# A two-layer graph attention kernel: scores of a chunk in two groups of 32 nodes, 640 slots each

## The chip, the cores and the metric

The kernel runs on one core of a Trainium2 chip. The metric is the time of one execution on the device in microseconds (us). TensorE (PE) multiplies matrices and loads their stationary operand (PEld), VectorE (DVE) and ScalarE (ACT) work element by element, GpSimd (POOL) issues the gathers, and SyncE (SP) issues most of the other transfers.

## The reference, cut to what matters

Two layers of attention over the edges of a graph with 6250 nodes of 128 features and 106250 edges, which come sorted by their destination. Layer normalisation of `x` plus the result stands at the end.

```python
def _transformer_conv(h, edge_attr, src, dst, Wq, bq, Wk, bk, Wv, bv, We, Ws, bs):
    q = (h @ Wq + bq).reshape(n, H, C)              # H = 2 heads of C = 64
    k = (h @ Wk + bk).reshape(n, H, C)
    v = (h @ Wv + bv).reshape(n, H, C)
    e = (edge_attr @ We).reshape(-1, H, C)          # 32 time features and 64 message features
    alpha = jnp.einsum('ehc,ehc->eh', q[dst], k[src] + e) / jnp.sqrt(C)
    a = segment_softmax(alpha, dst)                 # over all edges of one destination
    out = segment_sum((v[src] + e) * a[:, :, None], dst)
    return out.reshape(n, H * C) + h @ Ws + bs

edge_attr = concatenate([cos((node_vec[src] - edge_weight) * time_w + time_b), edge_attr_64])
h = _transformer_conv(x, edge_attr, ...)            # first layer
h = relu(batchnorm(h))
out = layernorm(x + _transformer_conv(h, edge_attr, ...))
```

## The kernel before

The sorted edges are cut into NC = 106 chunks. A chunk has CE = 1024 slots (T = 8 tiles of P = 128 edges) and a window of NN = 64 destination nodes, so NN nodes times H = 2 heads make 128 rows of scores. A plan at the start finds the first node and the first slot of each chunk, tests whether all chunks fit, and writes the flag `oki`; on it the program branches into `ordered` (measured here) or a general path.

`conv(c, ...)` runs twice (c = 0 and 1), each time as a software pipeline over rounds k, written out by hand in the loop at L937. In a round each step works on another chunk:

- `fetch(k + 4)` and `gather(k + 4)`: loads of the chunk's edge features into the tile `ff` and of its score tables `ftab` (SP's queue), and eight indirect gathers (POOL, L749), one for each tile of 128 edges, of source rows (`xv_d`, or `h_d` and `hn_d` in the second convolution) into `ff`.
- `turn_in(k + 1, u)`: PE turns the gathered rows (L799), in the first convolution also the edge features (L811); ACT copies them to `fft` and `fet`. In the second convolution the turned edge features are loaded from `et_d` instead. The first turn of a chunk waits for all eight gathers.
- `score(k, u)`: PE computes all 128 rows against 1024 slots in two halves of 512 (L822, L823) into `fps`. Slots of other nodes are masked by large codes in the tables.
- `lowest(k)` and `weigh(k)`: DVE takes the minimum of each row (L828), ACT the exponential (L835) into `fs`.
- `turn_weights(k - 1)`: PE turns the eight tiles of weights (L845), ACT copies them to `fpt` (L846).
- `gather_sums(k - 1)`: PE adds up weights times features, eight matmuls of 225 columns into `fpa` (L852).
- `divide(k - 2)`, `finish_turn(k - 2)`, `apply(k - 2)`, `finish(k - 2)`: division by the sum of weights (DVE), two turns (L872, L873) and a copy `fat` (L875), the value matrices (L882, L883 or L888, L889), and the end: the result's columns go to `hT` (L900), or in the second convolution the layer normalisation, whose rows `store` writes.
- `pull(extra, ...)`: one step of a generator `rest()`: in the first convolution the score tables of later nodes (`tables`, L627) and, when the last chunk of a block of 512 nodes is done, `pass_rows`, which turns that block of `hT` (L1015) and writes it to `h_d`; in the second convolution the tables of the second layer.

Each engine executes its instructions in the order in which they are issued. `ff` and `ftab` have six buffers, `fps`, `fpa` and `fpo` one each. Between the two convolutions all of `hT` must be done for the batch statistics; the second convolution's first gathers read `h_d`. Its chunk 105 ends with the store of the last rows.

Of the kernel before, what the change touches and what calls it, by code (L numbers as in the profile page):

```python
# [13 lines left out]
P = 128  # L14
# [33 lines left out]
NC = 106  # L48
EW = ED + 1

BITS = 8
# [609 lines left out]
def ordered(ctx: ExitStack, tc: tile.TileContext, pl, x, dst, edge_attr_64, conv2, bn_g, bn_b, out):  # L661
# [37 lines left out]
    def conv(c, extra, first_blocks=None):  # L699
# [13 lines left out]
        together = mybir.DependencyInfo(mybir.DependencyClass.Sync, mybir.DependencyReason.DATA)  # L713
        ets = [pl.xT[:EC, i * CE:(i + 1) * CE] for i in range(AHEAD + 2)]
        ch = {}
        norm = [None, None, None]
# [3 lines left out]
        def fetch(k):  # L720
            s = ch[k] = Plan()
            lo, hi = first(k)
            s.nb = nc.sync.value_load(pl.nbs[0:1, k:k + 1], min_val=lo, max_val=hi)
            sl = nc.sync.value_load(pl.sls[0:1, k:k + 1], min_val=0, max_val=E - CE)
            s.f = f = load.tile([P, T, FW], F32, name="ff")
            nc.sync.dma_start(f[:, :, 1 + D + TD:D + EW],
                              edge_attr_64[bass.ds(sl, CE), :].rearrange("(t p) d -> p t d", p=P))
            if c:
                nc.vector.memset(f[:, :, D + EW:1 + D + EW], 1.0)
            else:  # L730
                bits = small.tile([P, T, BITS], I32, name="fbits")
                nc.vector.tensor_tensor(bits, pl.dsts[:, :, k:k + 1].to_broadcast([P, T, BITS]),
                                        pl.bitm[:, None, :].to_broadcast([P, T, BITS]), OP.bitwise_and)
                nc.vector.tensor_scalar(f[:, :, D + EW:D + EW + BITS], bits, 0.0, None, op0=OP.is_equal)
                nc.vector.tensor_copy(f[:, :, D + EW + BITS:], bits)
            s.tab = load.tile([P, NN * H, 3 - c], F32, name="ftab")
            nc.sync.dma_start(s.tab, pl.tab_d[c][:, bass.ds(s.nb, NN)].rearrange("p n h w -> p (n h) w"))
            if c:
                s.z = load.tile([P, T, TD], F32, name="fz", bufs=AHEAD)
                nc.sync.dma_start(s.z, enc_d[k].rearrange("p (t d) -> p t d", d=TD))  # L740
                s.et = ets[k % len(ets)]
                nc.sync.dma_start(s.et, et_d[k])
                s.r = load.tile([NN, D], F32, name="fr", bufs=AHEAD + 3)
                nc.sync.dma_start(s.r, res_d[bass.ds(s.nb, NN), :])
# [70 lines left out]

        def score(k, u):

            s = ch[k]
            if u == 0:
                s.ps = p_s.tile([P, CE], F32, name="fps")  # L820
            w = slice(u * GE, (u + 1) * GE)
            nc.tensor.matmul(s.ps[:, w], s.tab[:, :, 0], s.ft[:, w], start=True, stop=False)  # L822
            nc.tensor.matmul(s.ps[:, w], s.tab[:EC, :, 1], s.et[:, w], start=False, stop=True)  # L823

        def lowest(k):
            s = ch[k]
            low = small.tile([P, 1], F32, name="flow")
            nc.vector.tensor_reduce(low, s.ps, AX.X, OP.min)  # L828
            s.bias = small.tile([P, 1], F32, name="fm")
            nc.vector.tensor_scalar(s.bias, low, HIGHEST, None, op0=OP.min)  # L830

        def weigh(k):
            s = ch[k]
            s.s = work.tile([P, CE], F32, name="fs")
            nc.scalar.activation(s.s, s.ps, AF.Exp, bias=s.bias, scale=-1.0)  # L835

        def turn_weights(k):

            s = ch[k]
            s.pt = work.tile([P, CE], F32, name="fpt")  # L840
            for u in range(2):
                pp = p_tr.tile([P, GE], F32, name="fppt", tag="tr")
                for t in range(4):
                    at = u * GE + t * P
                    nc.tensor.transpose(pp[:, t * P:(t + 1) * P], s.s[:, at:at + P], ident)  # L845
                nc.scalar.copy(s.pt[:, u * GE:(u + 1) * GE], pp)  # L846

        def gather_sums(k):
            s = ch[k]
            s.pa = p_a.tile([P, D + EW], F32, name="fpa")  # L850
            for t in range(T):
                nc.tensor.matmul(s.pa, s.pt[:, t * P:(t + 1) * P], s.f[:, t, 1:1 + D + EW], start=t == 0, stop=t == T - 1)  # L852

# [81 lines left out]

        with cs, tc.manual_schedule():
            for k in range(-AHEAD, NC + 3):  # L937
                def on(j):
# [5 lines left out]
                if k == -AHEAD and c:  # L944
                    first_blocks()
                if on(k):
                    score(k, 0)
                if on(k - 1):
# [4 lines left out]
                if on(k):  # L953
                    score(k, 1)
                if on(k - 2):
                    finish_turn(k - 2)
                if on(k):
                    lowest(k)
                if on(k + 1):
                    turn_in(k + 1, 0)  # L960
                if on(k - 2):
                    apply(k - 2)
                if on(k):
# [164 lines left out]
def tile_gnn_resnorm(ctx: ExitStack, tc: tile.TileContext, x, src, dst, edge_attr_64, edge_weight, node_vec,  # L1128
# [3 lines left out]
    E = src.shape[0]  # L1132
    step = -(-E // NC)
    keep = ctx.enter_context(tc.tile_pool(name="keep", bufs=1))
    made = ctx.enter_context(tc.tile_pool(name="made", bufs=1, space=bass.MemoryType.DRAM))
# [6 lines left out]
    with tc.tile_pool(name="plan", bufs=1) as pl, tc.tile_pool(name="planw", bufs=2) as mw, \  # L1142
# [3 lines left out]
        for r0, r1 in ((0, R // 16 * 16), (R // 16 * 16, R)):  # L1146
            nc.sync.dma_start(win[r0:r1], bass.AP(tensor=dst.tensor, offset=dst.offset + step * (r0 + 1) - (P - 1),
                                                  ap=[[step, r1 - r0], [1, P]]))
# [23 lines left out]
        tau_i = pl.tile([P, 1], I32, name="tau_i")  # L1172
        nc.gpsimd.iota(tau_i, pattern=[[0, 1]], base=step, channel_multiplier=step)
        lane_i = pl.tile([P, 1], I32, name="lane_i")
# [62 lines left out]
        nc.vector.tensor_scalar(span[:, 1], span[:, 1], float(CE), None, op0=OP.is_gt)  # L1237
        bad = pl.tile([1, 4], F32, name="bad")
        nc.vector.tensor_scalar(bad[:, 3:], ends[:, 0, NC - 2:NC - 1], N - NN + 0.5, None, op0=OP.is_gt)
        nc.vector.tensor_reduce(bad[:, 0:1], span, AX.XY, OP.add)  # L1240
# [97 lines left out]
```

## Time and profile before

| | |
|---|---|
| median of 14 runs | 2286.08 us (2283.77 to 2289.91) |
| the profiled execution | 2286.73 us, its span 2284.9 us |
| busy: PE, DVE, ACT, POOL | 2202.6, 1226.9, 1225.3, 1620.7 us |
| gathers of the first convolution (POOL) | first at 38.06, last at 1127.37 us |
| gathers of the second convolution (POOL) | first at 1181.08, last at 2244.96 us |
| score matmuls, L822 and L823, x1696 | 442.8 + 218.1 + 217.8 us busy |
| turns of weights, L845, x1696 | 220.0 us busy |
| sums, L852, x3392 | 681.9 us busy |

The span runs from the first instruction to the last; what lies around it makes the profiled execution 1.8 us longer. A logical matmul of 4-byte numbers appears as two instructions, a turn as one. The ends of matmuls are modelled and overlap the next start, so their pace is read from start to start. In a line of a timeline the columns are the start, the length, the engine, the line of the kernel, the operation, the tiles written and read with their shapes, how many in a row, and in brackets how long the engine had been idle and what released it. In a group of the page: the sum of busy time, the mean in ns, and the idle time before, with what ended most of it.

### The profile page before, as it was taken

Reading aid. Unit: us, or ns where it says so; the run is one execution under the profiler, and the core shown is the slowest. Engines: PE = TensorE matmul, PEld = TensorE weight load, DVE = VectorE, ACT = ScalarE, POOL = GpSimd, SP = SyncE. Lnnn points to the kernel's source line nnn. Section 1 sums busy time; section 2 is a strip of 40 time slices with the busy share of each in tenths; the row PEclk is TensorE's granted clock in tenths of the full one; section 3 lists DMA queues with packets and bytes.
Section 4 is the critical chain, followed back from the end, with each engine's and each line's share of the span. In section 5 each row is a group of like instructions: output and inputs, shape, how many; then the busy total and the mean of one; then the engine's idle time right before and its main releaser. Section 6 shows DMA issues by size and latency. Waiting matters only on the chain.

```text
span 2284.9 us, 39797 instructions
## 1 busy us (share of the span) xinstructions
PE 2202.6 (96%) x11586; PEld 1704.2 (75%) x11586; DVE 1226.9 (54%) x3738; ACT 1225.3 (54%) x1955; POOL 1620.7 (71%) x1717
## 2 busy tenths in 40 slices
PE   5999999999999999999979999999999999999997
PEld 3687878878887888888856777777777777777765
DVE  5576767676666666777735443344343334433333
ACT  3677777766566666555643343444444444444444
POOL 3777777767777777777527777777777777777772
PEclk8899999999999999999998999999999999999999
DMA  7666666656665666666539666666666766656561
GB/s 235 172 185 163 180 187 182 183 145 184 185 176 168 174 188 176 178 173 172 159 100 255 178 180 180 172 189 178 188 181 163 192 188 175 184 163 164 161 162 27
DMA packets 431119, 396.64 MB, mean 174 GB/s; under 512 B 279697, under 2 KB 375182, under 8 KB 427566
## 3 DMA queue, kind: packets, MB, share of 16 engines
q1 hardware_dynamic: 357680, 239.73, 38.3%
q0 software_dynamic: 54656, 113.07, 19.0%
q10 hardware_dynamic: 18558, 41.20, 5.2%
q8 instruction: 98, 1.61, 0.3%
q14 instruction: 127, 1.04, 0.2%
HBM read 277.19 MB, written 113.17 MB: 171 GB/s over the span
## 4 chain that ended last, share of the span: by engine, by line
PE 90%; DVE 3%; DMA 2%; issue 2%; POOL 2%; ACT 1%; SPq 0%; ACTq 0%; DVEq 0%; POOLq 0%
PE fpa L852 28%; PE fps L822 16%; PE fps L823 15%; PE fppt L845 8%; PE fpx L799 7%; PE fpg L627 4%; PE fpe L811 4%; PE fpo L888 2%; DVE fat L875 2%; POOL ff L749 2%; PE fpo L889 1%; PE fpo L882 1%; PE fpo L873 1%; PE fpo L872 1%; PE fpo L883 1%
## 5 line engine op out<-in xcount | busy, mean ns | idle before, releaser
L749 POOL DMA_INDIRECT ff<-xv_d,fsrcs x848 | 811.4, 957 | 305.8 <-issue 230.4
L749 POOL DMA_INDIRECT ff<-hn_d,fsrcs x824 | 781.5, 948 | 253.4 <-issue 221.9
L852 PE MATMUL fpa<-ff,fpt 128*128 128x225 f32 x3392 | 681.9, 353 | 0.0
L852 PEld LDWEIGHTS fpa<-ff,fpt 128*128 128x128 f32 x3392 | 634.6, 190 | 52.3 <-issue 48.5
L846 ACT COPY fpt<-fppt 128x512 f32<-128x512 f32 x424 | 228.2, 590 | 448.2 <-PE fppt L845 423.9
L822 PE MATMUL fps<-fft,ftab 128*128 128x512 f32 x848 | 442.8, 604 | 1.7 <-ACT fs L835 1.7
L806 ACT COPY fft<-fpx 128x512 f32<-128x512 f32 x418 | 243.3, 582 | 365.0 <-PE fpx L799 358.4
L875 DVE COPY fat<-fpo 128x256 f32<-128x256 f32 x212 | 90.1, 425 | 599.0 <-PE fpo L873 581.5
L835 ACT ACTIVATE fs<-fps,fm 128x1024 f32<-128x1024 f32 x212 | 236.4, 1115 | 76.4 <-DVE fm L830 69.8
L845 PEld LDWEIGHTS fppt<-fident,fs 128*128 128x128 f32 x1696 | 198.4, 140 | 104.8 <-issue 104.2
L799 PE MATMUL fpx<-fident,ff 128*128 128x128 f32 x1696 | 263.2, 278 | 13.9 <-ACT fo L631 5.3
L828 DVE TENSOR_REDUCE flow<-fps 128x1 f32<-128x1024 f32 x212 | 257.6, 1215 | 8.3 <-PE fps L823 8.3
L845 PE MATMUL fppt<-fident,fs 128*128 128x128 f32 x1696 | 220.0, 272 | 0.0
L823 PE MATMUL fps<-fxT,ftab 112*128 112x512 f32 x424 | 218.1, 595 | 0.4 <-DMA fxT<-et_d 0.4
L823 PE MATMUL fps<-fet,ftab 112*128 112x512 f32 x424 | 217.8, 595 | 0.0
L799 PEld LDWEIGHTS fpx<-fident,ff 128*128 128x128 f32 x1696 | 194.7, 142 | 27.0 <-ACT fo L631 7.1
L822 PEld LDWEIGHTS fps<-fft,ftab 128*128 128x128 f32 x848 | 166.7, 226 | 5.5 <-ACT fs L835 3.4
L823 PEld LDWEIGHTS fps<-fet,ftab 112*128 112x128 f32 x424 | 106.4, 251 | 76.1 <-issue 60.2
L823 PEld LDWEIGHTS fps<-fxT,ftab 112*128 112x128 f32 x424 | 83.8, 198 | 100.0 <-issue 97.8
L857 DVE TENSOR_SCALAR finv<-fpa 128x1 f32<-128x1 f32 x212 | 32.0, 151 | 211.0 <-issue 156.8
L774 DVE SCALAR_TENSOR_TENSOR farg<-fturns,farg 128x256 f32<-128x256 f32 x318 | 135.5, 426 | 10.9
L811 PE MATMUL fpe<-fident,ff 128*112 128x128 f32 x848 | 129.1, 275 | 1.5 <-DVE ff L786 1.5
(202 smaller groups left out, 2317.6 us busy)
## 6 DMA issues: line engine op xcount, KB each, us to landing
ff<-in_edge_attr SPq DMA_DIRECT2D x212, 256.0 KB
et_d<-fet SPq DMA_DIRECT2D x106, 448.0 KB
fxT<-et_d SPq DMA_DIRECT2D x106, 448.0 KB
ftab<-tab_d SPq DMA_DIRECT2D x106, 192.0 KB
tab_d<-fo ACTq DMA_DIRECT2D x13, 1536.0 KB
ff<-xv_d,fsrcs POOLq DMA_INDIRECT x848
enc_d<-fzs SPq DMA_DIRECT2D x106, 128.0 KB
ftab<-tab_d SPq DMA_DIRECT2D x106, 128.0 KB
```

What stands on the lines that cost most here:

```text
L749: nc.gpsimd.indirect_dma_start(out=f[:, t, (1 if c else 0):1 + D], out_offset=None, in_=(h_d if k < RAW else hn_d) if c else pl.xv_d, in_o ...
L799: turn = nc.tensor.transpose(px[:, t * P:(t + 1) * P], s.f[:, u * 4 + t, 1:1 + D], ident)
L806: nc.scalar.copy(s.ft[:, u * GE:(u + 1) * GE], px)
L811: nc.tensor.transpose(pe[:EC, t * P:(t + 1) * P], s.f[:, u * 4 + t, 1 + D:], ident)
L822: nc.tensor.matmul(s.ps[:, w], s.tab[:, :, 0], s.ft[:, w], start=True, stop=False)
L823: nc.tensor.matmul(s.ps[:, w], s.tab[:EC, :, 1], s.et[:, w], start=False, stop=True)
L828: nc.vector.tensor_reduce(low, s.ps, AX.X, OP.min)
L835: nc.scalar.activation(s.s, s.ps, AF.Exp, bias=s.bias, scale=-1.0)
L845: nc.tensor.transpose(pp[:, t * P:(t + 1) * P], s.s[:, at:at + P], ident)
L846: nc.scalar.copy(s.pt[:, u * GE:(u + 1) * GE], pp)
L852: nc.tensor.matmul(s.pa, s.pt[:, t * P:(t + 1) * P], s.f[:, t, 1:1 + D + EW], start=t == 0, stop=t == T - 1)
L875: nc.vector.tensor_copy(s.at, s.po)
```

## The change

The 64 nodes of a chunk are taken as two groups of 32. The first group is scored over slots 0 to 639, the second over slots 384 to 1023. Each group has 64 rows, which take 64 columns of TensorE: the first group's results stand on partitions 0 to 63 of `fps`, the second's on 64 to 127. `score` issues eight matmuls of 320 slots that alternate between the groups, in place of four of 512 slots with all 128 columns. Minimum and exponential work on 640 columns. `turn_weights` turns five tiles; four copies put each group's half of the turned tiles to its place among eight tiles of 128 columns, in one of two fixed buffers `pts`, whose other places are zeroed once at the start of each convolution, so that `gather_sums` stays as it is. The plan tests in addition that the border between the groups lies where both fit, which moves the turning of `dst` ahead of `oki`, and shifts the chunks' starts by 68 edges.

The order of a round changes: turning the weights of k - 1 comes first, both halves of the score follow together, `finish` works on chunk k - 3 in place of k - 2 and stands after the score, `finish_turn(k - 2)` comes after the turning in, and `apply(k - 2)` ends the round, after `gather_sums(k - 1)`. `ftab` and `fr` get one buffer more.

```diff
@@ conv @@
+        pts = [work.tile([P, T, P], F32, name=f"fpt{i}", bufs=1) for i in range(2)]
...
-            s.tab = load.tile([P, NN * H, 3 - c], F32, name="ftab")
+            s.tab = load.tile([P, NN * H, 3 - c], F32, name="ftab", bufs=AHEAD + 3)
...
-                s.r = load.tile([NN, D], F32, name="fr", bufs=AHEAD + 3)
+                s.r = load.tile([NN, D], F32, name="fr", bufs=AHEAD + 4)
...
-        def score(k, u):
+        def score(k):
             s = ch[k]
-            if u == 0:
-                s.ps = p_s.tile([P, CE], F32, name="fps")
-            w = slice(u * GE, (u + 1) * GE)
-            nc.tensor.matmul(s.ps[:, w], s.tab[:, :, 0], s.ft[:, w], start=True, stop=False)
-            nc.tensor.matmul(s.ps[:, w], s.tab[:EC, :, 1], s.et[:, w], start=False, stop=True)
+            s.ps = p_s.tile([P, 2, GE], F32, name="fps")
+            for u in range(2):
+                for i, (tab, of) in enumerate(((s.tab, s.ft), (s.tab[:EC], s.et))):
+                    for g in range(2):
+                        at = g * (CE - WE) + u * HE
+                        nc.tensor.matmul(s.ps[g * NN:(g + 1) * NN, u, :HE], tab[:, g * NN:(g + 1) * NN, i],
+                                         of[:, at:at + HE], start=i == 0, stop=i == 1)
...
-            nc.vector.tensor_reduce(low, s.ps, AX.X, OP.min)
+            nc.vector.tensor_reduce(low, s.ps[:, :, :HE], AX.XY, OP.min)
...
-            s.s = work.tile([P, CE], F32, name="fs")
-            nc.scalar.activation(s.s, s.ps, AF.Exp, bias=s.bias, scale=-1.0)
+            s.s = work.tile([P, WE], F32, name="fs")
+            nc.scalar.activation(s.s.rearrange("p (u e) -> p u e", u=2), s.ps[:, :, :HE], AF.Exp, bias=s.bias, scale=-1.0)
...
-            s.pt = work.tile([P, CE], F32, name="fpt")
-            for u in range(2):
+            s.pt = pts[k % 2]
+            for lo, hi in ((0, 4), (4, WT)):
                 pp = p_tr.tile([P, GE], F32, name="fppt", tag="tr")
-                for t in range(4):
-                    at = u * GE + t * P
-                    nc.tensor.transpose(pp[:, t * P:(t + 1) * P], s.s[:, at:at + P], ident)
-                nc.scalar.copy(s.pt[:, u * GE:(u + 1) * GE], pp)
+                for t in range(lo, hi):
+                    nc.tensor.transpose(pp[:, (t - lo) * P:(t - lo + 1) * P], s.s[:, t * P:(t + 1) * P], ident)
+                for g in range(2):
+                    nc.scalar.copy(s.pt[:, lo + g * (T - WT):hi + g * (T - WT), g * NN:(g + 1) * NN],
+                                   pp[:, :(hi - lo) * P].rearrange("p (t m) -> p t m", m=P)[:, :, g * NN:(g + 1) * NN])
...
         with cs, tc.manual_schedule():
+            for pt in pts:
+                nc.vector.memset(pt, 0.0)
             for k in range(-AHEAD, NC + 3):
...
-                if on(k):
-                    score(k, 0)
                 if on(k - 1):
                     turn_weights(k - 1)
                 place()
                 if on(k - 2):
                     divide(k - 2)
                 if on(k):
-                    score(k, 1)
-                if on(k - 2):
-                    finish_turn(k - 2)
+                    score(k)
+                if on(k - 3):
+                    finish(k - 3)
                 if on(k):
                     lowest(k)
                 if on(k + 1):
                     turn_in(k + 1, 0)
-                if on(k - 2):
-                    apply(k - 2)
                 if on(k):
                     weigh(k)
                 if on(k + 1):
                     turn_in(k + 1, 1)
                 if on(k - 2):
-                    finish(k - 2)
+                    finish_turn(k - 2)
...
                 if on(k - 1):
                     gather_sums(k - 1)
+                if on(k - 2):
+                    apply(k - 2)
@@ tile_gnn_resnorm @@
+        columns(flats[1], dsts)
+        split = pl.tile([1, 3, NC], F32, name="split")
+        nc.vector.tensor_scalar(split[:, 0], ends[:, 0, :NC], NH - 0.5, None, op0=OP.add)
+        for i, (t, op) in enumerate(((T - WT, OP.is_gt), (WT, OP.is_lt))):
+            nc.vector.tensor_copy(split[:, 1 + i], dsts[0:1, t])
+            nc.vector.tensor_tensor(split[:, 1 + i], split[:, 1 + i], split[:, 0], op)
+        nc.vector.tensor_reduce(bad[:, 4:], split[:, 1:], AX.XY, OP.add)
         tot = pl.tile([1, 1], F32, name="tot")
         nc.vector.tensor_reduce(tot, bad, AX.X, OP.add)
         nc.vector.tensor_scalar(oki, tot, 0.0, None, op0=OP.is_equal)
-        columns(flats[1], dsts)
         columns(flats[2], ew)
```

WT = 5 tiles, WE = 640 slots, HE = 320 and NH = 32 are new constants.

More of the change, by code (lines that the diff above doesn't have):

```diff
@@ L49 @@
 EW = ED + 1
+WT = 5
+WE = WT * P
+HE = WE // 2
+NH = NN // 2
 BITS = 8
@@ L851, in gather_sums @@
             for t in range(T):
-                nc.tensor.matmul(s.pa, s.pt[:, t * P:(t + 1) * P], s.f[:, t, 1:1 + D + EW], start=t == 0, stop=t == T - 1)
+                nc.tensor.matmul(s.pa, s.pt[:, t], s.f[:, t, 1:1 + D + EW], start=t == 0, stop=t == T - 1)
         def divide(k):
@@ L1133, in tile_gnn_resnorm @@
     step = -(-E // NC)
+    less = NC * step - E
     keep = ctx.enter_context(tc.tile_pool(name="keep", bufs=1))
@@ L1146, in tile_gnn_resnorm @@
         for r0, r1 in ((0, R // 16 * 16), (R // 16 * 16, R)):
-            nc.sync.dma_start(win[r0:r1], bass.AP(tensor=dst.tensor, offset=dst.offset + step * (r0 + 1) - (P - 1),
+            nc.sync.dma_start(win[r0:r1], bass.AP(tensor=dst.tensor, offset=dst.offset + step * (r0 + 1) - less - (P - 1),
                                                   ap=[[step, r1 - r0], [1, P]]))
@@ L1172, in tile_gnn_resnorm @@
         tau_i = pl.tile([P, 1], I32, name="tau_i")
-        nc.gpsimd.iota(tau_i, pattern=[[0, 1]], base=step, channel_multiplier=step)
+        nc.gpsimd.iota(tau_i, pattern=[[0, 1]], base=step - less, channel_multiplier=step)
         lane_i = pl.tile([P, 1], I32, name="lane_i")
@@ L1237, in tile_gnn_resnorm @@
         nc.vector.tensor_scalar(span[:, 1], span[:, 1], float(CE), None, op0=OP.is_gt)
-        bad = pl.tile([1, 4], F32, name="bad")
-        nc.vector.tensor_scalar(bad[:, 3:], ends[:, 0, NC - 2:NC - 1], N - NN + 0.5, None, op0=OP.is_gt)
+        bad = pl.tile([1, 5], F32, name="bad")
+        nc.vector.tensor_scalar(bad[:, 3:4], ends[:, 0, NC - 2:NC - 1], N - NN + 0.5, None, op0=OP.is_gt)
         nc.vector.tensor_reduce(bad[:, 0:1], span, AX.XY, OP.add)
```

## The prediction

> **What bounds the kernel now.** The page first: engine rows and the groups of the gathers.
>
> ```profile
> PE 2202.6 (96%) x11586; PEld 1704.2 (75%) x11586; DVE 1226.9 (54%) x3738; ACT 1225.3 (54%) x1955; POOL 1620.7 (71%) x1717
> L749 POOL DMA_INDIRECT ff<-xv_d,fsrcs x848 | 811.4, 957 | 305.8 <-issue 230.4
> L749 POOL DMA_INDIRECT ff<-hn_d,fsrcs x824 | 781.5, 948 | 253.4 <-issue 221.9
> ```
>
> PE is busy 96%, so shorter scores look like a gain in every round. POOL's 71% hides a second bound: most idle time before a gather is "issue", a wait for nothing visible. The timeline of POOL in the second convolution shows the beat:
>
> ```profile
> 1599.49 0.94 POOL L749 DMA_INDIRECT ff<-hn_d,fsrcs  x1 [0.30 <-issue]
> 1600.74 0.94 POOL L749 DMA_INDIRECT ff<-hn_d,fsrcs  x1 [0.30 <-issue]
> 1601.99 0.95 POOL L749 DMA_INDIRECT ff<-hn_d,fsrcs  x1 [0.30 <-issue]
> ```
>
> One gather per 1.25 us: 0.94 busy, 0.30 until the next. The same beat holds from 38 to 60 us, when PE has hardly started, so it is POOL's own. Eight gathers make a round of 10.0 us. Now PE's round, from its timeline in the first convolution:
>
> ```profile
> 600.88 3.21 PE L852 MATMUL fpa<-ff,fpt 128*128 128x225 f32 x16
> 603.92 1.02 PE L822 MATMUL fps<-fft,ftab 128*128 128x512 f32 x2
> 604.78 1.02 PE L823 MATMUL fps<-fet,ftab 112*128 112x512 f32 x2
> 605.64 1.04 PE L845 MATMUL fppt<-fident,fs 128*128 128x128 f32 x8
> 606.51 1.08 PE L822 MATMUL fps<-fft,ftab 128*128 128x512 f32 x2
> 607.43 1.02 PE L823 MATMUL fps<-fet,ftab 112*128 112x512 f32 x2
> ...
> 610.71 3.21 PE L852 MATMUL fpa<-ff,fpt 128*128 128x225 f32 x16
> ```
>
> Start to start it is 9.83 us; the blocks of `rest()` (0.86 us a matmul, about 58 us per convolution) raise the first convolution above 10.0. So the first is PE's, narrowly. In the second the fpa starts lie 9.38 apart where nothing is added: PE would need 106 x 9.38 + 47 = 1041 us, POOL ran 1181.1 to 2245.9 = 1065. The second is already POOL's. Where PE holds POOL up is in the waits of POOL, and where the end of a convolution is lost is in the timeline:
>
> ```profile
> POOL ff L749 <- PE fpa L852: 32.3, 39, 2.8
> ```
>
> ```profile
> 1127.37 0.94 POOL L749 DMA_INDIRECT ff<-xv_d,fsrcs  x1 [0.30 <-DMA ff<-xv_d,fsrcs]
> 1151.71 0.60 PE L799 MATMUL fpx<-fident,ff 128*128 128x128 f32 x4
> 1181.08 0.94 POOL L749 DMA_INDIRECT ff<-h_d,fsrcs  x1 [52.76 <-ACT fhT L1094]
> 2244.96 0.94 POOL L749 DMA_INDIRECT ff<-hn_d,fsrcs  x1 [0.30 <-issue]
> 2247.77 0.60 PE L799 MATMUL fpx<-fident,ff 128*128 128x128 f32 x4
> ```
>
> Of the 32.3 us, 39 x 0.30 are the usual beat; 20.6 are waits for a freed `ff`. The last chunk's rows are turned at 1151.71, 24.3 us after their last gather began; at the end of the second convolution that takes 2.8. So PE ends the first convolution 21.5 us behind. These two are what a shorter PE round can win; the rest is POOL's beat.
>
> **PE's round after the change.** Out: four score matmuls (two instructions each, start to start 0.43), 4 x 0.863 = 3.45 us, and three turns of 0.109 = 0.33. In: eight logical matmuls over 320 slots into 64 columns. At 0.43 us for 512 slots an instruction takes 0.267; sixteen one after another are S = 4.27. No row of before has matmuls in different column halves, so S is bounded by that and by complete overlap, 2.13. The halves alternate in PE's order; if an instruction of one half runs beside the next of the other, sixteen fit into nine steps: S = 2.40, which I take. The nearest rows are the 64-column matmuls of `apply`:
>
> ```profile
> 2229.13 0.63 PE L799 MATMUL fpx<-fident,ff 128*128 128x128 f32 x4 [0.85 <-DMA ff<-hn_d,fsrcs]
> 2229.68 0.20 PEld L888 LDWEIGHTS fpo<-fwv,fat 128*64 128x64 f32 x2 [0.17 <-issue]
> 2229.85 0.28 PE L889 MATMUL fpo<-fwe,fat 128*64 128x64 f32 x2
> 2230.09 0.28 PE L889 MATMUL fpo<-fwe,fat 128*64 128x64 f32 x2
> 2230.31 0.66 PE L799 MATMUL fpx<-fident,ff 128*128 128x128 f32 x4
> ```
>
> Four instructions pass between 2229.85 and 2230.09, 0.06 each, though each weight load lasts 0.10: loads run beside matmuls in 64 columns too. The turns before and after stand about 0.1 us off: two changes of shape, 0.2 a round. The round is S + 0.55 + 1.74 + 0.22 + 0.44 + 3.04 + 0.2 = S + 6.2: 8.6 instead of 9.8, and the first convolution 106 x 8.6 + 58 = 970 us of PE against 1062 of POOL. PE is ahead of POOL for any S up to about 3.2.
>
> The Trainium skill, "TensorE: Matmul & The Clock Gate", Part 3 (The mechanism), says that a weight load overlaps running matmuls only if its row group differs, and both halves here use all rows. By it sixteen loads of 0.1 would be bare, S = 4.0 and the change slower; the 0.06 pace above contradicts it, and no run yet shows it for two column halves. The same part reports 2.38 times for three column tiles; by that rate two would give, as an estimate, S near 2.7, with the same sum as 2.40.
>
> **The sum, against the profiled execution (run 2286.73, span 2284.9; median 2286.08, 0.65 lower).**
> 1. POOL's waits for `ff` go: 1127.4 becomes 1106.8. A further 8 us of slightly long gathers in the first convolution (957 against 948 ns) may or may not stay; I keep them.
> 2. The last chunk is turned 2.8 us later, at 1109.6, instead of 1151.7: -42.1.
> 3. From there to the last sums: before 20.0 us (1151.7 to `divide` at 1171.7). After: turns, sums and apply 5.4; 0.55 + 2.4 + 0.2 + 0.22 + 3.04 + 0.44 = 6.9; turns, copies, sums 5.1; together 17.4: -2.6.
> 4. From `divide` to the first gather of the second convolution: before 9.35. Two memsets of `fpt` now stand in DVE's order between `divide`'s steps; from 0.17 (128 columns) and 0.40 (406) one costs 0.9: +1.8. And the rows of block 11 (L1015), which PE turns before `apply(105)`, now need `finish(104)`'s write of `hT` from the same round; end of `fres` to turned row was 2.2 us (1174.9 to 1177.1). With DVE's copy and statistics (0.69 each) behind it, `finish(105)` comes 3 us later still. +4.8, bounds 0 and 7.
> 5. The second convolution stays 1065 us. Its tail: turn at 2247.8 to `divide` at 2271.2 was 23.5, with a 4.6 us gap in which ACT did a table load and `finish(103)` before `fpt`'s copies (2261.6 to 2266.2). Now the copies stand first: about 18.2. `finish(104)` moves into the last round, and its DVE steps wait for ACT in front of `fat(105)`: +1.6. Net -3.7, bounds 0 and -6.
>
> Sum: -42.1 - 2.6 + 4.8 - 3.7 = -43.6; 2286.7 - 43.6 - 0.7 = **2242**.
>
> **Edits at nothing, and their cover.** The reduction shrinks by 384 of 1024 columns (1.215 us; about 0.4 less), the exponential likewise; four smaller copies replace two (512: 0.58, 128: 0.28, so 2 x 0.38 + 2 x 0.23 = 1.2 against 1.2): DVE and ACT are 54% busy and neither sets the end. The dst columns now precede the flag `oki` (27.6 to some 32 us), on which SP and POOL branch; the first gather waits for `xv_d`, written until about 37, which covers it; uncovered it costs at most 5. The first pair of memsets delays DVE, not POOL. On SP the `ftab` load of chunk k+4 still waits for a `finish` of the same round (one buffer more, one round later), now earlier in DVE's order; the queue behind it holds `enc_d`, `hT`, `et_d`, none wanted within a round except `hT`: the rows of a finished block are turned in the round of its last `finish`, a stall of up to 2.5 us every eighth round, inside PE's 1.4 us of slack per round. `ff` is freed about 20 us before POOL asks, so a late PE round stops nothing. POOL's order is unchanged.
>
> **Rivals.**
> Slower: the halves run one after another. Then S = 4.27 and PE's round grows by 0.44 (without changes of shape) to 0.64. First convolution 47 to 68, plus 5 at its end; second 106 x (9.82 to 10.02) + 47 = 1088 to 1109 against 1065: 24 to 45. Together 76 to 118, about 2383. It decides from S = 3.55, where PE's round is what it was. For it: no row shows two halves at once. Against: the alternating order, the hidden loads.
> In between: S of 3.2 to 3.55 gives back part of item 2: 2250 to 2288, say 2265.
> POOL's beat is no floor: with PE as the bound, 212 rounds less 1.2 each give 2030. Against it: the beat is 1.25 whether anyone waits or not.
> The change doesn't do its work: if a node of one group lies outside its 640 slots, the program takes its general path, which no run here times. From the reference's `dst` the border between the groups lies at slot 482 to 583 in all 106 chunks, inside 384 to 640; under 0.01.
>
> **How the numbers follow.** Main case 0.76: S between 2.13 and 3.2 is half of the open interval and all of it gives the same time; alternating halves and hidden loads take it to three quarters. In between 0.06, two thirds of it faster; serial halves 0.13; something unnamed, slower or equal, 0.03; POOL not a floor 0.02. Main case's own range: 2242 less 8 (long gathers) and 6 (items 4 and 5) is 2228; plus 6 for items 4 and 5 and 4 for step 3 is 2252. To hold 8 in 10 the range takes in the case in between: 2228 to 2288. A difference under 0.2% (4.6 us) can't be told from none. Faster 0.76 + 0.04 + 0.02 = 0.82, same 0.03, slower 0.15.
>
> **What would show it.** Right: gathers 1.25 apart in both convolutions, POOL's waits for fpa gone, PE with idle time before L799's turns "<-DMA ff", score instructions of the two halves starting together, the last gather of the first convolution near 1107 and the first of the second near 1141. Wrong: eight score matmuls at 0.53 us each and PE still full (serial); POOL's beat below 1.2; or the last turn of the first convolution more than 5 us behind its gather.

## The result, and the profile after

The changed kernel takes 2261.59 us (median; 2259.75 to 2263.0), the kernel before 2285.69 beside it: ratio 0.9895, 95% interval 0.9885 to 0.9904. It is 24.1 us faster; 43.6 were forecast, at 2242. The profiled execution took 2260.43 us with a span of 2258.6, so 26.3 us of span have to be found. The runs e5 to e8 come from a set in which the kernel before took 2846.6 us and not 2286, so they can only be read against that.

The page's engine row and its groups of the gathers (line, engine, operation, tiles, count | busy us, mean ns | idle before, and what ended most of it):

```profile
PE 1977.9 (88%) x12646; PEld 1557.5 (69%) x12646; DVE 1151.2 (51%) x3748; ACT 1096.4 (49%) x2379; POOL 1625.0 (72%) x1717
L755 POOL DMA_INDIRECT ff<-xv_d,fsrcs x848 | 815.2, 961 | 287.3 <-issue 217.3
L755 POOL DMA_INDIRECT ff<-hn_d,fsrcs x824 | 782.1, 949 | 255.1 <-issue 229.8
```

PE lost 225 us of busy time and the span 26: PE is no longer the bound. POOL's gathers take what they took, and its waits for `fpa`, 32.3 us before, are three of the usual beat (us in all, times, longest):

```profile
POOL ff L755 <- PE fpa L861: 0.9, 3, 0.3
```

A round of PE in its timeline:

```profile
600.39 0.79 PE L830 MATMUL fps<-fft,ftab 128*64 128x320 f32 x4
601.01 0.71 PE L830 MATMUL fps<-fet,ftab 112*64 112x320 f32 x4
601.56 0.71 PE L830 MATMUL fps<-fft,ftab 128*64 128x320 f32 x4
602.10 0.71 PE L830 MATMUL fps<-fet,ftab 112*64 112x320 f32 x4
602.74 0.66 PE L805 MATMUL fpx<-fident,ff 128*128 128x128 f32 x4
```

Sixteen score instructions pass in 602.74 - 600.39 = 2.35 us: S was taken as 2.40. Now the ends of the convolutions, from the timelines of POOL and PE: the last gather of the first, the turn of its last chunk, the first gather of the second, the last of all, and the last turn:

```profile
1112.82 0.94 POOL L755 DMA_INDIRECT ff<-xv_d,fsrcs  x1 [0.30 <-issue]
1127.82 0.66 PE L805 MATMUL fpx<-fident,ff 128*128 128x128 f32 x4
1157.67 0.94 POOL L755 DMA_INDIRECT ff<-h_d,fsrcs  x1 [43.92 <-DVE fshift L1073]
2223.59 0.94 POOL L755 DMA_INDIRECT ff<-hn_d,fsrcs  x1 [0.30 <-issue]
2226.36 1.06 PE L805 MATMUL fpx<-fident,ff 128*128 128x128 f32 x8 [2.06 <-issue]
```

The last chunk is still turned 15.0 us after its last gather began; 2.8 was forecast. With the lines shown of before, the span falls into stretches:

| stretch | before | after | difference | forecast |
|---|---|---|---|---|
| start to the first gather | 38.06 | 40.41 | +2.35 | 0 |
| first to last gather of the first convolution | 1089.3 | 1072.4 | -16.9 | -20.6 |
| last gather to last turn | 24.3 | 15.0 | -9.3 | -21.5 |
| last turn to `divide(105)` | 20.0 | 16.9 | -3.1 | -2.6 |
| `divide(105)` to the first gather of the second | 9.35 | 12.9 | +3.6 | +4.8 |
| first to last gather of the second | 1063.9 | 1065.9 | +2.0 | 0 |
| last gather to the end | 39.9 | 35.0 | -4.9 | -3.7 |

Of the 17.3 us that are missing, 12.2 stand in one row. Where they go is in the waits of DVE (line waited for: us in all, times, longest):

```profile
DVE frel L773 <- DMA ff<-xv_d,fsrcs: 207.3, 78, 6.2
```

L773 is the first line of `encode()`. In round k it takes chunk k+3 and, in DVE's order, stands there until that chunk's last gather has landed; what stands behind it on DVE waits too. So DVE does not get past its part of a round before the gather of a chunk that PE turns only two rounds later. PE's own waits show how it is held (its weight loads, which stand ahead of its matmuls, from 550 to 1060 us of the changed kernel):

```profile
PEld fpo L881 <- DVE fres L908: 19.1, 18, 2.2
PEld fpe L817 <- DVE fhr L1026: 14.2, 9, 2.4
PEld fpe L817 <- DVE fbits L738: 10.2, 5, 3.0
```

`finish_turn` waits for `fa` and for `fpo`, which `fres` frees; the turns of the edge features wait for a buffer that DVE frees when it has read `fpg` (L638, just ahead of `fbits`, or L1026). All of these stand behind `encode()` in DVE's order. From 640 us on no sine of ACT (L787) runs between such an `encode()` and the wait behind it, so this hold does not go through ACT. Turning that into a number for each chunk, start of its first turn less start of its last gather, from the timelines (means over chunks):

| kernel | chunks 10 to 29 | 50 to 99 | chunk 105 | second convolution, 50 to 99 |
|---|---|---|---|---|
| before | 19.8 | 26.1 | 24.3 | 9.3 |
| after | 9.9 | 17.7 | 15.0 | 4.1 |

In the changed kernel the lag steps from 10 to 18 where `encode()` goes from chunk k+2 to k+3 (SINGLE = 40), and it is 4 where nothing is encoded.

### The profile page after: what moved, and what is told of

Its sections match the earlier page's. It is cut to its first block, busy times and chain, and to the rows that moved or that the text cites. A ratio compares the mean times of both kernels' runs of the same rounds, so it can differ in the third digit from the quotient of the medians.

```text
span 2258.6 us, 42609 instructions
## 1 busy us (share of the span) xinstructions
PE 1977.9 (88%) x12646; PEld 1557.5 (69%) x12646; DVE 1151.2 (51%) x3748; ACT 1096.4 (49%) x2379; POOL 1625.0 (72%) x1717
## 5 line engine op out<-in xcount | busy, mean ns | idle before, releaser
L854 ACT COPY fpt<-fppt 128x256 f32<-128x256 f32 (+1 forms) x848 | 185.8, 305 | 359.2 <-PE fppt L852 334.3
L830 PE MATMUL fps<-fft,ftab 128*64 128x320 f32 x1696 | 318.7, 452 | 0.0
L836 DVE TENSOR_REDUCE flow<-fps 128x1 f32<-128x640 f32 x212 | 174.1, 821 | 213.4 <-PE fps L830 208.5
L843 ACT ACTIVATE fs<-fps,fm 128x640 f32<-128x640 f32 x212 | 168.8, 796 | 47.9 <-DVE fm L838 46.8
L830 PEld LDWEIGHTS fps<-fft,ftab 128*64 128x64 f32 x1696 | 117.2, 153 | 84.5 <-issue 26.9
L852 PE MATMUL fppt<-fident,fs 128*128 128x128 f32 x1060 | 156.8, 278 | 2.3 <-DVE fo L638 0.8
L830 PE MATMUL fps<-fxT,ftab 112*64 112x320 f32 x848 | 154.0, 438 | 0.8 <-DMA fxT<-et_d 0.8
L830 PE MATMUL fps<-fet,ftab 112*64 112x320 f32 x848 | 150.6, 432 | 0.0
L817 PEld LDWEIGHTS fpe<-fident,ff 128*112 128x112 f32 x848 | 99.5, 138 | 72.5 <-issue 24.8
L818 ACT COPY fet<-fpe 112x512 f32<-112x512 f32 x212 | 126.5, 597 | 35.9 <-PE fpe L817 33.3
```

Of the source, the lines that this page charges most:

```text
L817: nc.tensor.transpose(pe[:EC, t * P:(t + 1) * P], s.f[:, u * 4 + t, 1 + D:], ident)
L818: nc.scalar.copy(s.et[:, u * GE:(u + 1) * GE], pe[:EC])
L830: nc.tensor.matmul(s.ps[g * NN:(g + 1) * NN, u, :HE], tab[:, g * NN:(g + 1) * NN, i], of[:, at:at + HE], start=i == 0, stop=i == 1)
L836: nc.vector.tensor_reduce(low, s.ps[:, :, :HE], AX.XY, OP.min)
L843: nc.scalar.activation(s.s.rearrange("p (u e) -> p u e", u=2), s.ps[:, :, :HE], AF.Exp, bias=s.bias, scale=-1.0)
L852: nc.tensor.transpose(pp[:, (t - lo) * P:(t - lo + 1) * P], s.s[:, t * P:(t + 1) * P], ident)
```

## The experiments

### Where the missing 12 us of the last chunk went

**e1_late.** The lookahead goes back to k+2 for the last rounds alone:

```diff
+    LATE = 100
-  for j in (k + 2,) if k < SINGLE else ... else (k + 3,):
+  for j in (k + 2,) if k < SINGLE or k > LATE else ... else (k + 3,) if k < LATE else ():
-      if j < SINGLE + 3:
+      if j < SINGLE + 3 or k > LATE:
```

> From round 100 on, encode() takes chunk k+2 instead of k+3, one chunk at a time; all else as in the changed kernel. Theory: the last chunk is turned 12 to 15 us behind its gather because DVE, in order, stands in encode(105) in round 102 until the gather of chunk 105 has landed, and ACT's sine and PE's turns stand behind it. Then the wait moves one round later, a round of 8 to 9 us leaves the end of the first convolution, turn_in(105) starts near 1119 to 1121 instead of 1127.8, and the time falls from 2261.6 to about 2253 (2251 to 2256). Rival: the lag is the work of PE's last rounds or latency of the transfers; then the turn stays near 1127 and the time within 2 us of 2261.6.

Measured: 2259.63 us, ratio 0.9884 (0.9868 to 0.9901), no different from the changed kernel; last turn 14.0 us behind. The expectation failed, and the trace says how: from round 100 on PE ran without a wait, 8.49 us from turn to turn, and was still late, because the lag that was there goes away by no more than POOL's round less PE's, 10.05 - 8.49 = 1.56 us a round (chunks 102 to 105: 18.7, 17.0, 15.5, 14.0). The lag had also grown just before, from 16.8 at chunk 100 to 20.3 at chunk 101: in round 99 PE waited for a write of `hT`, and the sums behind it took 4.89 us instead of 3.21, at half the clock (0.51 from 1083.9 to 1087.3 us).

```profile
1083.13 0.30 PE L1026 MATMUL fpg<-fident,fhT 128*128 128x128 f32 x1 [2.66 <-DMA fhT<-fres]
1083.27 4.89 PE L863 MATMUL fpa<-ff,fpt 128*128 128x225 f32 x16
```

Without that jump the same pace would have led, as an estimate, to 16.8 - 5 x 1.56 = 9.0. So the rival was right for those last rounds, and this run leaves open what made the lag in the rounds before. That asks for the short lookahead in all rounds.

**e5_single, e9_single_again.** One number:

```diff
-    SINGLE = 40
+    SINGLE = NC
```

> SINGLE is 106 instead of 40, so that encode() takes chunk k+2, one at a time, in all rounds of the first convolution; nothing else. In the changed kernel the turn of a chunk starts 9 to 10 us behind the start of its last gather while encode() takes chunk k+2 (chunks 0 to 39), 16 to 18 us while it takes chunk k+3, and 3 to 5 us in the second convolution, which encodes nothing. Theory: the place of encode() in the round, not PE's work, sets how far PE follows POOL, so the lag of the last chunk falls from 15.0 to 8 to 10, and the stretch from the last gather to the first of the second convolution from 44.9 to 38 to 40: 2255 to 2257. Rival: the two table loads of ACT in every round, which the pairs had halved, cost more than that; then gathers stretch or the lag stays over 13, and the time is 2261 or more. Second rival: PE is behind by its own work; then lag 15 and 2261.

In the set with 2846.6 us e5_single took 3084.42 us (ratio 1.0825, 1.0781 to 1.0869). Its waits show PE holding POOL up, so it decides nothing about a lag that only PE's slack can show:

```profile
POOL ff L755 <- PE fpa L861: 709.4, 143, 27.8
```

> The edit of e5_single once more: that set of runs came from a chip on which the kernel before took 2846.6 us, with PE's granted clock at 0.94 instead of 0.99, and PE held back in stretches of 5 to 7 us, so that PE and not POOL set both convolutions. Theory as there: encode() in the round, not PE's work, sets how far PE follows POOL; where the kernel before takes 2286, the lag of the last chunk is 8 to 10 us instead of 15.0, the stretch from the last gather to the first of the second convolution 38 to 40 us instead of 44.9, and the time 2255 to 2257 (ratio 0.986 to 0.987). Rival: ACT's table loads in every round cost more than that (2261 or more); second rival: PE is behind by its own work (lag 15, 2261).

Measured: 2254.54 us against 2288.22 before, ratio 0.9851 (0.9837 to 0.9866), below the changed kernel's interval. Its timelines:

```profile
1113.13 0.94 POOL L755 DMA_INDIRECT ff<-xv_d,fsrcs  x1 [0.30 <-issue]
1121.07 0.66 PE L805 MATMUL fpx<-fident,ff 128*128 128x128 f32 x4
1151.12 0.94 POOL L755 DMA_INDIRECT ff<-h_d,fsrcs  x1 [37.04 <-DVE fshift L1073]
```

| kernel | chunks 10 to 29 | 50 to 99 | chunk 105 | second convolution, 50 to 99 |
|---|---|---|---|---|
| e9_single_again | 9.6 | 8.8 | 7.9 | 4.2 |
| e10_best | 9.8 | 8.7 | 8.3 | 4.2 |
| e12_scores | 11.2 | 20.6 | 18.6 | 4.6 |

The lag is 8.8 on the mean of chunks 50 to 99, 7.9 at the last chunk, and the stretch between the two convolutions' gathers 37.99 instead of 44.85: the theory's 8 to 10, 38 to 40, and 2255. ACT's table loads, 105 at L787 instead of 74, do not show in the time. DVE's wait at `frel` falls from 207.3 to 144.9 us, and from 550 to 1060 us no wait of PE's weight loads is put down to DVE any more. The edit moves `encode()` and, with it, ends the pairs of sines, and no run parts the two; but in the changed kernel PE was held behind `encode()` on DVE with no sine in between. So the place of `encode()` set PE's lag.

### The smaller steps

**e2_memset.** The tiles are made outside `conv()` and set once:

```diff
-        pts = [work.tile([P, T, P], F32, name=f"fpt{i}", bufs=1) for i in range(2)]
+    pts = [const.tile([P, T, P], F32, name=f"fpt{i}") for i in range(2)]     # ahead of conv()
-            for pt in pts:
+            for pt in pts if c == 0 else ():
```

> The two fpt tiles are allocated once outside conv() and set to zero in the first convolution alone. Theory (the prediction's item 4): the two memsets of 0.91 us stand in DVE's order between the steps of divide(105) and delay the first gather of the second convolution by 1.8 us: about 2259.8, and divide(105) to the first gather 11.1 instead of 12.9. Rival: they lie beside the wait for the transfer of fhT that follows, and the stretch stays at 12.9.

Measured: 2257.59 us, ratio 0.9871 (0.9854 to 0.9887). DVE's timeline at the last `divide`, first of the changed kernel, then of e2_memset:

```profile
1144.75 0.16 DVE L866 TENSOR_SCALAR finv<-fpa 128x1 f32<-128x1 f32 x1 [2.62 <-PE fpa L861]
1145.30 0.91 DVE L947 MEMSET fpt<- 128x1024 f32 x1 [0.39 <-issue]
1146.24 0.16 DVE L867 RECIPROCAL finv<-finv 128x1 f32<-128x1 f32 x1
1146.57 0.91 DVE L947 MEMSET fpt<- 128x1024 f32 x1 [0.16 <-issue]
1147.40 0.33 DVE L869 TENSOR_SCALAR fa<-fpa,finv 128x225 f32<-128x225 f32 x1
```

```profile
1144.88 0.16 DVE L867 TENSOR_SCALAR finv<-fpa 128x1 f32<-128x1 f32 x1 [2.62 <-PE fpa L862]
1145.08 0.16 DVE L868 RECIPROCAL finv<-finv 128x1 f32<-128x1 f32 x1
1145.28 0.45 DVE L870 TENSOR_SCALAR fa<-fpa,finv 128x225 f32<-128x225 f32 x1
```

`fa` begins 0.40 us after `finv` instead of 2.65, and the first gather of the second convolution comes 10.8 us after `finv` instead of 12.9: of 2.25 us, 2.1 are on the path. The stretch shows this; the two times differ by 4 with intervals that touch.

**e3_rows.**

```diff
-   while at_round[0] < 3 + max(k for k in range(NC) if first(k)[0] < (b0 + 1) * GE):
+   while at_round[0] < 4 + max(k for k in range(NC) if first(k)[0] < (b0 + 1) * GE):
```

> The rows of a finished block are turned a round later (4 instead of 3 in rest()), so that PE no longer turns rows of block 11 before apply(105) and waits there for the write of hT. Theory (item 4): 3 us leave the stretch from divide(105) to the first gather, given back in part by the turned rows, their copy and statistics behind the last chunk: net -1 to -3, about 2259.5. Rival: the stretch is held by the last write of hT alone, and nothing changes, or it gets longer by the moved rows (up to +2).

Measured: 2262.92 us; `divide(105)` to first gather 13.5 instead of 12.9. The rival held. The stop in front of `apply(105)` is gone, and `fres` of chunk 105 begins 5.98 us after `finv` instead of 6.98, but DVE's copy and statistics of block 11 (0.69 each) now stand behind it, a transfer into `ff` (0.42) is issued ahead of the write of `hT` on SP's queue, and PE's last turned row comes 3.9 us after that `fres` instead of 2.3. In that trace PE also ran at half its clock from 1102.0 to 1108.8 us and the last lag was 18.0 instead of 15.0, which is 3.0 of the 3.4 us between the two spans.

**e4_start.**

```diff
         columns(flats[2], ew)
+        ok = nc.values_load(oki[0:1, 0:1], min_val=0, max_val=1)
     got.nbs, got.sls = nbs, sls
-    ok = nc.values_load(oki[0:1, 0:1], min_val=0, max_val=1)
```

> Only one thing moves: the load of the flag oki into registers is recorded behind the plan's last steps, so that on SP's queue it stands behind the fourth write of xv_d, not ahead of it. Theory: in the changed kernel SP waited 11.6 us for oki in front of that write, and the first gather came at 40.4 instead of 38.1. Now the write starts when ACT's copy is done, near 29.5, and the first gather comes between 36 and 38.4: -2 to -4.4 us, about 2258.5. Rival: the first gather hangs on the flag itself (oki ready near 33, then the branch and the instructions behind it) or on later transfers of the queue: 40 again, 2261.6.

Its reason is in the waits of SP's queue, in the changed kernel, and in the queue's timeline, the fourth write of `xv_d`:

```profile
SPq L1318 <- DVE oki L1314: 11.6, 1, 11.6
```

```profile
33.95 0.32 SPq L534 DMA_DIRECT2D xv_d<-fxrows  x1
```

ACT's copy for that write had ended at 29.44. Measured: 2259.73 us, ratio 0.9879 (0.9863 to 0.9896), not told apart from the changed kernel; first gather at 39.45, later than expected. In that run ACT's copy itself ended at 31.14, 1.7 late; from its end to the first gather it is 8.3 us instead of 11.0. In e10_best, with the same edit, ACT's copy ended at 28.03, 1.4 early, and the first gather comes 9.0 us behind it, at the expected time:

```profile
28.06 0.32 SPq L534 DMA_DIRECT2D xv_d<-fxrows  x1
36.98 0.96 POOL L756 DMA_INDIRECT ff<-xv_d,fsrcs  x1 [25.53 <-PE fpx L656]
```

The six other runs without the edit and beside a kernel before of 2286 us have it between 39.99 and 40.93. Read from the end of ACT's copy, the flag's load on SP cost the start 2 to 3 us.

**e6_clamp.** Some 77 gathers of the first convolution came 0.1 to 0.3 us late.

```diff
-   nc.vector.tensor_scalar(arg, arg, -3 * HALF_PI, HALF_PI, op0=OP.max, op1=OP.min)
+   nc.vector.scalar_tensor_tensor(arg, arg, -3 * HALF_PI, top, op0=OP.max, op1=OP.min)
```

> The last step of encode() (two clamps of 128x256 values, one source) is written as an instruction with two sources, the second a tile that holds the upper bound; the values are the same. In the changed kernel the first convolution has 77 gathers that come 1.35 to 1.55 us after the one before, not 1.25, and of such gathers between 450 and 850 us 70% lie beside this instruction, against 8% of the others. Theory: this form of DVE instruction holds POOL up; then most of the long gathers go, the first convolution's gathers take 1065 to 1067 us instead of 1072, and the time is about 2256. Rival: it only stands where a gather lands, and the long gathers come from something else (the transfers of the round, any DVE instruction): their number stays within a fifth, gathers 1071 to 1073 us, time 2261.

It ran in the set with 2846.6 us (3073.3 us, ratio 1.0799), so its time says nothing here. In its trace about two thirds of the long gathers lie beside the rewritten instruction and 7% of the others, about as with the old form: nothing speaks for the form of the instruction as the cause. In e9_single_again, where `encode()` stands elsewhere, some 80 gathers are as long. What makes them long stays open; the first convolution's gathers took 1072.4 us, and 847 beats of 1.25 would be 1058.8, so they and the slightly long ones are worth some 14 us.

### Which bound, and which part of the change

**e7_seven, e11_seven_again.**

```diff
-  for t in range(T)]
+  for t in range(T - 1 if c and k >= RAW else T)]
+  if c and k >= RAW:
+      ch[k].rows.append(nc.sync.dma_start(f[:, T - 1, 1:1 + D], hn_d[:P, :]))
```

> In the second convolution, from chunk 3 on, the eighth gather of a chunk is replaced by a plain transfer of 128 rows from SP's queue, so those slots hold other rows than they should; 103 gathers fewer on POOL, PE's work the same. Theory: POOL's beat of 1.25 us sets both convolutions; then the second one's gathers take 1065.9 less 103 x 1.25 = 129 us, 937 (935 to 950), and the time is about 2135. PE's own round is 8.5 us where it does not wait, below 8.77. Rival: PE or the work around it sets the second convolution; then the gathers come apart, POOL waits for ff, and the time stays above 2240.

e7_seven ran in the set with 2846.6 us, where PE was the bound (2956.11 us, ratio 1.0393), and decides nothing.

> The edit of e7_seven once more, where the kernel before takes 2286 us (in the set of e7_seven it took 2846.6): in the second convolution, from chunk 3 on, the eighth gather of a chunk is a plain transfer of 128 rows from SP's queue, so those slots hold other rows than they should. Theory: POOL's beat sets the second convolution, so its gathers take 937 us (935 to 950) instead of 1065.9, and the time is about 2133 (2130 to 2146). Rival: PE or the work around it sets it: the gathers come apart, POOL waits for ff, and the time stays above 2240. In between: PE's own round of 8.2 to 8.5 us with rest()'s blocks in the first half is close below the new beat of 8.77, so that PE holds POOL up there: 2140 to 2170.

Measured: 2134.86 us, ratio 0.9343 (0.9327 to 0.9358). This kernel leaves out one gather in each of 103 chunks, so its result is not the reference's, and the second convolution's gathers took 935.1 us instead of 1065.9: 1.27 us for each one left out. POOL's timeline there keeps the beat:

```profile
1600.24 0.95 POOL L755 DMA_INDIRECT ff<-hn_d,fsrcs  x1 [0.30 <-issue]
1601.50 0.94 POOL L755 DMA_INDIRECT ff<-hn_d,fsrcs  x1 [0.30 <-issue]
1602.74 0.94 POOL L755 DMA_INDIRECT ff<-hn_d,fsrcs  x1 [0.30 <-issue]
```

The beat is the floor, and PE's round fits under 8.77 us too. So the changed kernel would gain nothing more from a shorter PE round, save at the ends.

**e8_halves.**

```diff
-  for u in range(2):
-      for i, (tab, of) in enumerate(...):
-          for g in range(2):
+  for g in range(2):
+      for u in range(2):
+          for i, (tab, of) in enumerate(...):
```

> The eight score matmuls are issued group after group (four for the first column half, then four for the second) instead of half by half in turn; same work. Theory: two matmuls run side by side only where the next instruction goes to the other column half; then sixteen instructions one after another take 4.27 us instead of 2.3, PE's round grows from 8.5 to 10.4 us, above POOL's 10.0, PE sets both convolutions, and the time is between 2300 and 2370. Rival: the pace does not depend on the order (a half is fast by itself, or PE reorders): scores 2.3 us and 2261. In between: scores of 2.3 to 3.8 us leave the time at 2261 to 2270, since POOL's round covers them.

It ran in the set with 2846.6 us (3048.46 us, ratio 1.0696); its scores can still be read from PE's timeline, here at the full clock (1.00 from 707.3 to 710.8 us):

```profile
707.31 0.79 PE L830 MATMUL fps<-fft,ftab 128*64 128x320 f32 x2
707.93 0.70 PE L830 MATMUL fps<-fet,ftab 112*64 112x320 f32 x2
708.47 0.79 PE L830 MATMUL fps<-fft,ftab 128*64 128x320 f32 x4
709.01 0.79 PE L830 MATMUL fps<-fet,ftab 112*64 112x320 f32 x4
709.64 0.70 PE L830 MATMUL fps<-fft,ftab 128*64 128x320 f32 x2
710.18 0.70 PE L830 MATMUL fps<-fet,ftab 112*64 112x320 f32 x2
710.81 0.44 PE L805 MATMUL fpx<-fident,ff 128*128 128x128 f32 x2
```

Two instructions of one half take 0.54 us; four of both halves, in the middle, take 0.54 too. By records, the second half's first matmuls run beside the first half's last ones, though they are issued behind them, and the rest stands alone: 3.50 us in all, between the 2.35 of the alternating order (e5_single, of the same set, has it too: 508.44 to 510.79) and 4.27. The alternation is what makes S small, as the prediction assumed, and the expectation's 4.27 was too high.

**e12_scores.** New scores and layout, the order of the round as before the change (the scores whole, after `divide`; `apply` and `finish` of chunk k-2 back between and behind the turns; the conditions `if on(...)` are left out here):

```diff
                 score(k)
-                finish(k - 3)
+                finish_turn(k - 2)
                 lowest(k)
                 turn_in(k + 1, 0)
+                apply(k - 2)
                 weigh(k)
                 turn_in(k + 1, 1)
-                finish_turn(k - 2)
+                finish(k - 2)
...
                 gather_sums(k - 1)
-                apply(k - 2)
```

> The new scores and the turned weights' layout in the old order of a round (score(k) whole where its second half stood, finish_turn(k-2) behind it, apply(k-2) between the two halves of turn_in, finish(k-2) behind them). Theory: the shorter scores carry what POOL's waits and the last chunk's lag give, the order only the tails: first convolution's gathers 1072, last chunk's lag 14 to 17, the tail behind the last gather 38 to 40 us instead of 35.0 (39.9 in the kernel before), time 2262 to 2267. Rival: in the old order PE waits for fat and the sums of the round before, and its round stays near 9.8, so that the lag grows towards 24 and the waits for ff come back: 2275 or more.

Measured: 2268.94 us, ratio 0.9928 (0.9911 to 0.9945). The gathers of the first convolution took 1072.5, as forecast, the last lag was 18.6 and the tail 41.3 us, both a little over. So the scores with their layout give 16.9 of the 24.1 us, the order the other 7. Between the two profiled spans it is 8.7: 3.6 in the last lag, 1.7 to `divide` and 6.3 in the tail, less 1.0 that the order costs behind `divide` (11.9 against 12.9) and 1.8 in the second convolution.

**e10_best.** e9's number, e2's tiles and e4's load together.

> Three edits together: SINGLE 106 (encode() takes chunk k+2 in all rounds), the fpt tiles set to zero once, and the flag's load behind the fourth write of xv_d. Theory: their gains add, 6 (lag) + 1.8 (memsets) + 1 (start): 2252 to 2254 where the kernel before takes 2286 (ratio 0.985 to 0.986), and the stretch between the two convolutions' gathers near 37. Rival: one wait takes the place of another (the write of hT and its turn, 2 us each, stand behind all of it), so that no more comes out than by the best of them alone: 2256.

Measured: 2249.66 us, ratio 0.9833 (0.9818 to 0.9848); 36.10 us between the two convolutions' gathers. It is 12 us below the changed kernel and a little better than expected, by the start (36.98). This version is faster than both kernels.

## Why the prediction was right, and where it was too large

The sign is right and the main case came about: S is 2.35 and POOL's beat is the bound. Its time did not: 2261.6 lies outside the main case's own 2228 to 2252. It is inside the stated range because that was widened to 2288 for a case, S of 3.2 to 3.55, that did not occur; in this respect it was luck. And one of the signs that the prediction had named for being wrong came true, a last turn of the first convolution more than 5 us behind its gather. The gain was 24 where 43.6 were forecast.

- *POOL's beat as the bound.* Shown by e11_seven_again. The rival in which it was no floor (2030) is out.
- *PE's round, S = 2.40.* 2.35 measured, and 8.49 us a round where PE did not wait, 8.6 forecast. The slower rival, halves one after another, fell: e8_halves shows both paces side by side. The Trainium skill, "TensorE: Matmul & The Clock Gate", Part 3 (The mechanism), says that a weight load overlaps running matmuls only where its row group differs, though it also lets a load into the background weight buffer be pulled ahead. Both halves use all rows, so by the first statement alone S would be, as an estimate, 4.0. The 2.35 us contradict that for two column halves.
- *Item 1, POOL's waits, 20.6.* The waits on `fpa` are gone, but the gathers' stretch fell by 16.9: that term was 3.7 too large, and its long gathers remain (e6_clamp, e9_single_again: cause open).
- *Item 2, "the last chunk is turned 2.8 us later".* This is the step that failed. The 2.8 were taken from the end of the second convolution, where no `encode()` runs. In the first, its wait for chunk k+3 keeps PE 17.7 us behind POOL, most of two rounds, on the mean of chunks 50 to 99. The prediction compared PE's round with POOL's and took it that a faster PE would catch up; it had no term for what ties PE to POOL through DVE. The kernel before hid that, since there PE was slower still and DVE waited at `frel` for 18.3 us in all instead of 207.3. 15.0 instead of 2.8 is 12.2 us. e9_single_again moves the wait by a chunk and gets 7.1 of them back; with `encode()` still in the round, 7.9 remain.
- *Item 3.* -3.1 against -2.6: right.
- *Item 4.* +3.6 against +4.8. The memsets were sized right (1.8; 2.1 by e2_memset). The 3 us for rows ahead of `apply(105)` were too much: 1.0 by e12_scores, and e3_rows gets nothing by taking them away.
- *Item 5.* The second convolution +2.0 against 0, the tail -4.9 against -3.7: right.
- *The stall at a finished block's rows "inside PE's 1.4 us of slack per round".* In e1_late it was 2.66 us in round 99, with half the clock behind it; the lag rose by 3.5 us, and at 1.56 a round that takes more than two rounds to come back.
- *The move of `oki` "at nothing".* The cover that was named, the writes of `xv_d`, was itself behind the flag: SP loads the flag ahead of the fourth write. +2.35 at the start; e4_start and e10_best show it.

## What to carry to other kernels

When the slower engine of two gets faster, ask what else ties it to the other: an element engine that takes its work in order, and waits in it for data of a later step, holds every engine behind it at that step's pace, and a slower engine hides this. Read a lag from the same stage, not from one that looks alike but leaves a step out. Where a scalar is loaded for a branch, look at what stands behind it on that engine's own queue.

## What the runs showed of the hardware

- Two chains of fp32 matmuls into different column halves ran side by side at 0.54 us for four instructions of 320 slots, the time of two in one half; only where instructions of both halves stand near each other in PE's order (e8_halves: 3.50 us for sixteen, 2.35 when they alternate).
- PE's mean granted clock fell from 0.986 to 0.96 (0.949 to 0.972 in the experiments beside a kernel before of 2286), and the clock records show how: the clock is full or half, and it is at half in 34 stretches, 181.8 us together, against 7 and 67.9 us before. From 85 to 1110 and from 1215 to 2215 us the kernel before has no such stretch and the changed one 25, each behind 3.4 us in which PE was busy for less than half. e11_seven_again, whose shorter rounds leave PE few pauses in the second convolution, has 2 there instead of 16. So a pause of PE can cost twice, though no run varies the pause alone: the lag jumps at such places, here from 17.3 us at chunk 64 to 22.3 at chunk 65 (stretch and its length; busy PE, PEld, DVE, ACT and POOL with their instructions; clock, DMA share, GB/s):

```profile
713.50:716.90 3.40, 1.57 (x12) 0.76 (x8) 3.16 (x9) 0.58 (x1) 2.72 (x3) 1.00 0.62 146
716.90:723.70 6.80, 5.83 (x19) 4.72 (x20) 5.74 (x18) 3.19 (x5) 5.08 (x6) 0.50 0.40 106
```

- In the set with 2846.6 us the kernel before had a clock of 0.94, the variants of the changed kernel 0.85 to 0.91, and they were the slower ones, by 4 to 8%. In e5_single's trace the clock is at half in 149 stretches, 913.6 of 3083.2 us. The changed kernel itself did not run there, and why PE pauses so often there is open. It need not lie in the chip: the record gives the same chip number for e11 and e12, beside a kernel before of 2285.84. What is a gain beside a kernel before of 2286 us need not be one there.
